# A gated recurrence inside a four-layer kernel: the PSUM tiles of its gates merged, three small jobs moved to other places and engines

## The chip, the cores and the metric

The kernel runs on one core of a Trainium2 chip. The metric is the device time of one execution in microseconds (us). A core has TensorE (PE, matrix products; PEld is its weight load), VectorE (DVE), ScalarE (ACT), GpSimd (POOL) and SyncE (SP, which issues transfers). Each engine takes its own instructions in the order in which the program gives them, and waits for other engines by semaphores.

## The reference

Four residual layers over an activation `x` of 16 x 256 x 512 (batch, time, features) with a mask `cond` of 16 x 512: `x` plus an attention (8 heads), plus a depthwise convolution of 16 taps whose taps are the mask's rows, plus a recurrence, plus an attention (16 heads). The change touches the recurrence, a GRU over 256 steps:

```
def cell(h, x):
    gi = x @ W_ih + b_ih
    gh = h @ W_hh + b_hh
    i_r, i_z, i_n = jnp.split(gi, 3, axis=-1)
    h_r, h_z, h_n = jnp.split(gh, 3, axis=-1)
    r = jax.nn.sigmoid(i_r + h_r)
    z = jax.nn.sigmoid(i_z + h_z)
    n = jnp.tanh(i_n + r * h_n)
    h_new = (1.0 - z) * n + z * h
    return (h_new, h_new)
```

A step needs the state of the step before, so the 256 steps run one after another. The state is 16 x 512 and W_hh is 512 x 1536, all in float32.

## The kernel before

The first attention runs up to about 480 us of the profile, the recurrence from there to about 1567 us, the second attention after it. Within the recurrence the order on every engine is that of the Python code (`manual_schedule`). The waits between engines are not in the code: the tile framework derives them from the tiles that each instruction reads and writes, and from their order.

**A step** (`step`, L1223). Features lie on partitions; `state_part` (L1209) multiplies the old state by one gate's share of W_hh. For each of four chunks `f` of 128 features, four products with 32 output partitions each (`j`) run side by side in the array. So one gate is 16 products, which the trace shows as 32 matmul instructions, and one step has three gates. Their sums go to three PSUM tiles `pr`, `pn`, `pz` of 128 x 128, of which there are two sets (`sets`, L1173): one set serves two steps, since the input's products for two steps are made at once. In program order a step is:

1. PE: r products into `pr`; ACT: sigmoid of `pr` (L1237); DVE: transposes the result (`rT`, L1238).
2. PE: n products into `pn`; DVE: transposes `pn` (`hT`, L1240), multiplies it with r (`rn`, L1241), adds the input's share (`pre`, L1242); ACT: tanh (L1244).
3. PE: z products into `pz`; DVE: transposes `pz` in two halves (`zT`, L1249); ACT: 1 - z in two halves (`omz`, L1251); DVE: `d`, `m`, and the new state into `hist` (L1252, L1254, L1255), in halves too, so that the next step's first products can begin with the first half.

**What the loop adds to a step** (L1291 to L1312), after it in program order:

- `input_part` (L1187): the products of the input with W_ih for the r and z gates of a later pair of steps, added into the other set: 16 products of 128 columns a step.
- After every second step, three ACT copies (L1299) put the biases into the set just used.
- `turned_part` (L1195): a sixteenth of the n gate's input products for the next 16 steps (a "part"), four products of 256 columns a step, into a PSUM tile `pt`. Two buffers of the pool `psw` are there for it; every fourth step ACT takes one to SBUF (L1207).
- `take` (L1179): in the last four steps of a part, one ACT copy each brings a later part's input into order (L1185, 64 copies in all).
- `add_part` (L1216): once a part is done, two DVE additions write its states plus its input into `xT` (L1221, 32 in all).
- `conv` (L555): two taps of the convolution layer a step on DVE (L558, 384 instructions in all), but in the step that holds the additions.
- After step 8, `projection` (L346) transposes the second attention's three weight matrices: 12 transpositions on PE (L343), each copied out of PSUM by ACT (L354), through the pool `psw`.

The lines outside of the recurrence that the prediction uses: L618 to L629 in the setup, where one PSUM tile `ps` ("places") is written by PE in columns 0 to 63 (L621), read there by DVE (L624), then written in columns 64 to 79 (L627); and L1520 with L1529 in the second attention, where PE writes two halves of one bank of the tile `SM` (through the helper at L1457) and ACT reads them half by half. `SM` is made as eight banks of 512 float32 columns.

Of the kernel before, what the change touches and what calls it, by code (L numbers as in the profile page):

```python
# [264 lines left out]
def tile_kernel(ctx: ExitStack, tc: tile.TileContext, x, cond, Wq0, Wo0, W_ih, W_hh, b_ih, b_hh,  # L265
# [35 lines left out]
    whh = cpool.tile([P, NT, 3 * T], F32, tag="whh", name="whh")  # L301


    gbias = cpool.tile([72, P], F32, tag="gbias", name="gbias")
    nbias = cpool.tile([P, NT], F32, tag="nbias", name="nbias")

    wih = cpool.tile([P, NT, 3 * T], F32, tag="wih", name="wih")
# [38 lines left out]
    def projection(psm, wnat, flat, padded, R, dk, name):  # L346

        if padded is not None:
            nc.vector.memset(padded, 0.0)
        for oc in range(KC):  # L350
            for kc in range(KC):
                ps = transposed(psm, wnat, oc, kc, f"{name}t{oc}{kc}")
                if flat is not None:
                    nc.scalar.copy(flat[:, kc, oc * P : (oc + 1) * P], ps[:, 0:P])  # L354
                if padded is not None:
                    nh = P // dk
                    dst = padded[:, kc, oc * nh * R : (oc + 1) * nh * R].rearrange("p (h r) -> p h r", r=R)
                    nc.vector.tensor_copy(dst[:, :, 0:dk], ps[:, 0:P].rearrange("p (h i) -> p h i", i=dk))
# [274 lines left out]
    bi = b_ih.rearrange("(g f j i) -> g j f i", g=3, f=NT, i=32)  # L633
    bh = b_hh.rearrange("(g f j i) -> g j f i", g=3, f=NT, i=32)
    for at_row, src, g in ((0, bi, GATE_R), (4, bh, GATE_R), (36, bh, GATE_N), (64, bi, GATE_Z), (68, bh, GATE_Z)):
        nc.sync.dma_start(out=gbias[at_row : at_row + 4].rearrange("r (f i) -> r f i", i=32), in_=src[g])
    nc.sync.dma_start(out=nbias, in_=b_ih[2 * T : 3 * T].rearrange("(f p) -> p f", p=P))

    together = nc.values_load(flag[0:1, 0:1], min_val=0, max_val=1)
# [514 lines left out]
    with ExitStack() as es:  # L1154
        gp = es.enter_context(tc.tile_pool(name="gru", bufs=2))
        gw = es.enter_context(tc.tile_pool(name="gruw", bufs=1))
        psg = es.enter_context(tc.tile_pool(name="psg", bufs=1, space=PSUM))
        psw = es.enter_context(tc.tile_pool(name="psw", bufs=2, space=PSUM))
        yw.append(gw.tile([P, NT, B, WIN], F32, tag="yw2", name="yw2"))


# [8 lines left out]

        sets = [[psg.tile([P, P], F32, tag=f"{n}{i}", name=f"p{n}{i}") for n in "rnz"] for i in range(2)]  # L1173
        bias = gw.tile([P, 3, P], F32, tag="bias", name="bias")

        def gates(w, f, j):
            return w[:, f].rearrange("p (g c j i) -> p g j c i", g=3, c=NT, i=32)[:, :, j]

        def take(p, f):  # L1179


            if f == 0:
                parts[p] = gp.tile([P, NT, PART, B], F32, tag="xw", name=f"xw_{p}", bufs=3)
            lo = p % 2 * PART
            nc.scalar.copy(parts[p][:, f], yw[p // 2 % 3][:, f, :, lo : lo + PART].rearrange("p b s -> p s b"))  # L1185

        def input_part(k, f, g):  # L1187

            xw, s0 = parts[2 * k // PART], 2 * k % PART
            x2 = xw[:, f, s0 : s0 + 2].rearrange("p s b -> p (s b)")  # L1190
            for j in range(4):
                nc.tensor.matmul(sets[k % 2][0 if g == GATE_R else 2][32 * j : 32 * j + 32].rearrange("p (f i) -> p f i", i=32),  # L1192
                                 lhsT=x2, rhs=gates(wih, f, j)[:, g], start=False, stop=False, skip_group_check=True)

        def turned_part(p, q):  # L1195

# [19 lines left out]
        def add_part(p, q):  # L1216
            dst = xT[:, :, :, p * PART + q : (p + 1) * PART : 2]
            at_col = B * ((q + 1) % 2)
            src = hist[p % 2][:, q::2, :, at_col : at_col + B].rearrange("p s f b -> p f b s")
            lo = p % 2 * PART  # L1220
            nc.vector.tensor_tensor(dst, yw[p // 2 % 3][:, :, :, lo + q : lo + PART : 2], src, ALU.add)  # L1221

        def step(t):  # L1223
            pr, pn, pz = sets[t // 2 % 2]
            before, slot = state(t - 1)
            after, _ = state(t)

            def mine(tl):
                return tl.rearrange("p (f r) -> p f r", r=2 * B)[:, :, B * (t % 2) : B * (t % 2) + B]

            def sbuf(name, shape):
                return gp.tile(shape, F32, tag=name, name=f"{name}_{t}")

            r, rT, hT, zT = (sbuf(n, [P, P]) for n in ("r", "rT", "hT", "zT"))
            rn, pre, nn, omz, d, m = (sbuf(n, [P, NT, B]) for n in ("rn", "pre", "nn", "omz", "d", "m"))
            state_part(slot, pr, GATE_R)
            nc.scalar.activation(r, pr, AF.Sigmoid)  # L1237
            nc.vector.transpose(rT, r)  # L1238
            state_part(slot, pn, GATE_N)
            nc.vector.transpose(hT, pn)  # L1240
            nc.vector.tensor_tensor(rn, mine(hT), mine(rT), ALU.mult)  # L1241
            nc.vector.tensor_tensor(pre, rn, turned[t // PART][:, :, t % PART], ALU.add)  # L1242
            state_part(slot, pz, GATE_Z)
            nc.scalar.activation(nn, pre, AF.Tanh)  # L1244


            halves = [slice(h * NT // 2, (h + 1) * NT // 2) for h in range(2)]
            for h in range(2):
                nc.vector.transpose(zT[:, h * P // 2 : (h + 1) * P // 2], pz[:, h * P // 2 : (h + 1) * P // 2])  # L1249
            for f in halves:  # L1250
                nc.scalar.activation(omz[:, f], mine(zT)[:, f], AF.Sigmoid, scale=-1.0)  # L1251
            nc.vector.tensor_tensor(d, nn, before, ALU.subtract)  # L1252
            for f in halves:
                nc.vector.tensor_tensor(m[:, f], d[:, f], omz[:, f], ALU.mult)  # L1254
                nc.vector.tensor_tensor(after[:, f], m[:, f], before[:, f], ALU.add)  # L1255
# [3 lines left out]

        taps = [(f, k, w * WIN) for w in range(EARLY // 2, D // WIN) for f in range(NT) for k in range(TAPS)]  # L1260
        parts, turned, added = {}, {}, 0

        n = TAPS - 1 + EARLY * PART
        room = yw[2].rearrange("p f b s -> p (f b s)")
# [2 lines left out]
        with tc.manual_schedule(engines=ENG):  # L1267

            nc.scalar.activation(gp.tile([P, NT], F32, tag="table", name="table", bufs=1), nbias, AF.Sigmoid)
            nc.gpsimd.tensor_copy(xs[:, :, TAPS - 1 :], xT[:, :, B - 1, 0 : EARLY * PART])  # L1270
            for w in range(1, EARLY):
                for _, _, f in early(B - 1, w, xs, products):
                    f()
            for t in hist:
                nc.gpsimd.memset(t, 0.0)
            nc.vector.tensor_copy(hist[1][:, PART - 1, :, 0:B], condT)
            for k in range(2):
                for ps, base in zip(sets[k], (0, 32, 64)):
                    nc.tensor.matmul(ps, lhsT=cst("gsel")[base : base + 8], rhs=gbias[base : base + 8], start=True, stop=True)
            for i, ps in enumerate(sets[0]):  # L1280
                nc.scalar.copy(bias[:, i], ps)
            for f in range(NT):
                take(0, f)
            xparts = [(f, g) for f in range(NT) for g in (GATE_R, GATE_Z)]
            for f, g in xparts:
                input_part(0, f, g)
            for q in range(PART):
                turned_part(0, q)
            for f in range(NT):
                take(1, f)  # L1290
            for t in range(D):  # L1291
                step(t)
                p, q = divmod(t, PART)
                if t + 2 < D:
                    for f, g in xparts[4 * (t % 2) : 4 * (t % 2) + 4]:
                        input_part(t // 2 + 1, f, g)
                    if t % 2:
                        for i, ps in enumerate(sets[t // 2 % 2]):
                            nc.scalar.copy(ps, bias[:, i])  # L1299
                if p + 1 < D // PART:  # L1300
                    turned_part(p + 1, q)
                if p + 2 < D // PART and q >= 12:
                    take(p + 2, q - 12)
                for _ in range(2):
                    if added // 2 < p:
                        add_part(*divmod(added, 2))
                        added += 1
                    elif taps:
                        conv(*taps.pop(0))
                if t == 8:  # L1310
                    for wnat, flat, name in zip(wnats, (wq3T, wk3T, wv3T), ("wq3", "wk3", "wv3")):
                        projection(psw, wnat, flat, None, R3, DK3, name)  # L1312
            for q in range(2):
                add_part(D // PART - 1, q)

# [429 lines left out]
```

## Time and profile before

| | us |
|---|---|
| median of three runs (lowest, highest) | 2416.81 (2415.17, 2427.05) |
| the profiled execution | 2425.97 |
| its span | 2424.2 |
| in it: from the first r sigmoid (L1237) to the last | 494.28 to 1563.81 |
| a step, r sigmoid to r sigmoid, median of 255 | 4.06 |
| the longest, step 8 to step 9 (the 12 transpositions) | 13.59 |
| busy time of PE, DVE, ACT, POOL between 494 and 1567 us | 1045.7, 870.7, 359.4, 0.0 |

In the profile's lines "engine line op out<-in shapes xcount" names a group of instructions; in the timeline the first two columns are the start and the length in us, and a bracket at the end tells how long the engine was idle before and which instruction ended the wait.

### The profile page before, as it was taken

How to read it: one execution, taken by the hardware profiler on the slowest of the kernel's cores; microseconds unless marked ns; L12 is line 12 of the kernel's file. 1: busy time of each engine (PE TensorE's matmuls, PEld its weight loads, DVE VectorE, ACT ScalarE, POOL GpSimd, SP SyncE). 2: the span in 40 equal slices, each digit the busy share in tenths (PEclk: the TensorE clock that was granted, in tenths of full speed). 3: DMA queues.
4: the chain of work that ended last, by engine and by line, in shares of the span. 5: the costliest groups of instructions: out<-in, count | busy, mean ns of one | idle time of the engine just before them, and what ended most of it. 6: DMA issues, size and time to landing. Idle time of an engine off the chain costs nothing.

```text
span 2424.2 us, 105987 instructions
## 1 busy us (share of the span) xinstructions
PE 2217.7 (91%) x47074; PEld 1451.9 (60%) x47074; DVE 1677.4 (69%) x4611; ACT 997.8 (41%) x2648; POOL 420.7 (17%) x428
## 2 busy tenths in 40 slices
PE   5999999499999999999999999749999999999994
PEld 3555554278988898888988888623333333333331
DVE  2378778768888888888888655626555666566661
ACT  3555554233333333333333333215545555455552
POOL 3244433300000000000000000140332224222213
PEclk8999999699999999999999999969999999999997
DMA  6223322400000000000000000010111111111101
GB/s 198 72 79 106 83 70 66 152 4 4 5 4 5 4 5 4 4 5 4 5 4 5 5 4 4 4 42 16 37 42 32 31 43 43 32 31 38 32 21 40
DMA packets 70172, 83.97 MB, mean 35 GB/s; under 512 B 28808, under 2 KB 48842, under 8 KB 69700
## 3 DMA queue, kind: packets, MB, share of 16 engines
q1 hardware_dynamic: 60484, 60.09, 8.6%
q0 software_dynamic: 9216, 16.96, 2.3%
q8 instruction: 373, 6.11, 1.1%
q14 instruction: 99, 0.81, 0.1%
HBM read 48.58 MB, written 35.98 MB: 35 GB/s over the span
## 4 chain that ended last, share of the span: by engine, by line
issue 46%; PE 45%; DMA 2%; DVE 2%; another core or an unknown queue 1%; POOL 1%; ACT 1%; SPq 1%; POOLq 0%; DVEq 0%; ACTq 0%
PE smC L1457 10%; PE smC L1584 8%; PE smA L830 6%; PE smC L1616 6%; PE smC L1641 5%; PE smA L984 3%; PE smA L1014 3%; PE smA L941 2%; PE smC L1507 1%; DVE nmC L1591 1%; PE smA L856 1%; DMA backA<-result,goto 1%; PE smA L883 1%; PE smA L917 1%
## 5 line engine op out<-in xcount | busy, mean ns | idle before, releaser
L1591 DVE TENSOR_REDUCE nmC<-smC 128x2 f32<-128x576 f32 x512 | 364.9, 752 | 243.4 <-PE smC L1584 193.4
L1627 ACT ACTIVATE wih<-smC 128x1024 f32<-128x1024 f32 x256 | 252.3, 1023 | 146.9 <-PE smC L1616 132.8
L1213 PE MATMUL pr<-whh,hist 128*32 128x128 f32 x8192 | 284.0, 275 | 11.9 <-DVE hist L1255 6.7
L1213 PE MATMUL pz<-whh,hist 128*32 128x128 f32 x8192 | 283.6, 273 | 2.3 <-issue 2.3
L1213 PE MATMUL pn<-whh,hist 128*32 128x128 f32 x8192 | 280.8, 273 | 0.0
L1213 PEld LDWEIGHTS pr<-whh,hist 128*32 128x32 f32 x8192 | 222.1, 110 | 97.0 <-DVE hist L1255 43.8
L558 DVE SCALAR_TENSOR_TENSOR yw<-xT,condT,yw 128x512 f32<-128x512 f32 x360 | 269.4, 748 | 6.8
L1213 PEld LDWEIGHTS pz<-whh,hist 128*32 128x32 f32 x8192 | 240.1, 110 | 4.2 <-issue 3.7
L1192 PE MATMUL pr<-wih,xw 128*32 128x128 f32 x4096 | 230.0, 274 | 11.1 <-issue 6.1
L1213 PEld LDWEIGHTS pn<-whh,hist 128*32 128x32 f32 x8192 | 239.2, 110 | 0.1
L1584 PE MATMUL smC<-kC,qC 32*128 32x288 f32 x2048 | 203.8, 460 | 31.2 <-ACT qC L1557 17.4
L1192 PE MATMUL pz<-wih,xw 128*32 128x128 f32 x4096 | 230.4, 274 | 2.0 <-issue 1.1
L1584 PEld LDWEIGHTS smC<-kC,qC 32*128 32x128 f32 x2048 | 86.1, 186 | 232.4 <-DVE nmC L1591 93.5
L1244 ACT ACTIVATE nn<-pre 128x64 f32<-128x64 f32 x256 | 65.7, 257 | 387.6 <-DVE pre L1242 387.6
L1237 ACT ACTIVATE r<-pr 128x128 f32<-128x128 f32 x256 | 71.1, 278 | 293.3 <-PE pr L1213 293.3
L1445 POOL MEMSET pbC<- 128x512 f32 x4 | 2.3, 616 | 1088.0 <-issue 1088.0
L1681 POOL TENSOR_TENSOR aC<-aC,pbC 128x512 f32<-128x512 f32 x64 | 81.6, 1282 | 591.0 <-DMA pbC<-sums 413.5
L1204 PE MATMUL pt<-xw,wih 128*32 128x256 f32 x2048 | 172.8, 382 | 0.1
L1616 PE MATMUL smC<-qC,kC 32*128 32x512 f32 x1024 | 162.9, 648 | 6.0 <-ACT e3C L1624 4.6
L1192 PEld LDWEIGHTS pr<-wih,xw 128*32 128x32 f32 x4096 | 146.9, 110 | 15.5 <-issue 14.8
L1192 PEld LDWEIGHTS pz<-wih,xw 128*32 128x32 f32 x4096 | 148.3, 110 | 6.1 <-issue 6.0
L313 POOL DMA_INDIRECT table<-xT,togo x128 | 128.3, 1002 | 89.6 <-ACT xT L860 59.9
(184 smaller groups left out, 3468.8 us busy)
## 6 DMA issues: line engine op xcount, KB each, us to landing
xA<-in_x_dram SPq DMA_DIRECT2D x16, 512.0 KB
pbC<-sums SPq DMA_DIRECT2D x256, 32.0 KB
out_dram<-oC SPq DMA_DIRECT2D x32, 256.0 KB
table<-zeros SPq DMA_DIRECT2D x16, 288.0 KB
pbA<-totals SPq DMA_DIRECT2D x120, 36.0 KB
xsA<-table SPq DMA_DIRECT2D x16, 256.0 KB
result<-ocA SPq DMA_DIRECT2D x16, 256.0 KB
xsC<-table SPq DMA_DIRECT2D x16, 256.0 KB
```

The source lines that it names most:

```text
L313: one = nc.gpsimd.indirect_dma_start(tables[b], bass.IndirectOffsetOnAxis(togo[:, f, b : b + 1], 0), xT[:, f, b], None, bounds_check=ROOM ...
L558: nc.vector.scalar_tensor_tensor(acc, xT[:, f, :, lo : lo + WIN], condT[:, f, k : k + 1], xT[:, f, :, t0 : t0 + WIN] if k == 0 else acc, A ...
L830: nc.tensor.matmul(to[r : min(n, r + R)], lhsT=left[:, r : min(n, r + R)], rhs=right, start=start, stop=stop, skip_group_check=True)
L1192: nc.tensor.matmul(sets[k % 2][0 if g == GATE_R else 2][32 * j : 32 * j + 32].rearrange("p (f i) -> p f i", i=32), lhsT=x2, rhs=gates(wih, ...
L1204: nc.tensor.matmul(ps[32 * j : 32 * j + 32], lhsT=wih[:, kc, 2 * T + fo * P + 32 * j : 2 * T + fo * P + 32 * j + 32], rhs=parts[p][:, kc]. ...
L1213: nc.tensor.matmul(ps[32 * j : 32 * j + 32].rearrange("p (f i) -> p f i", i=32), lhsT=slot[:, f], rhs=gates(whh, f, j)[:, g], start=False, ...
L1457: nc.tensor.matmul(to[R3 * j : R3 * j + R3], lhsT=left[:, R3 * j : R3 * j + R3], rhs=right, start=start, stop=stop)
L1584: nc.tensor.matmul(SM[:, st[j].i, 0:ROOM], lhsT=Q[qt.i][R * j : R * j + R, qc * P : (qc + 1) * P], rhs=K[kt.i][R * j : R * j + R, 0:ROOM], ...
L1591: nc.vector.tensor_reduce(NM[nm.i][:, qc, lo : lo + len(some)], SM[:, some[0] : some[-1] + 1, 0:ROOM], AX.X, ALU.max, negate=True)
L1616: nc.tensor.matmul(SM[:, st[j].i], lhsT=K[kt.i][r, kc * P : kc * P + P], rhs=Q[qt.i][r, :], start=True, stop=True)
L1627: nc.scalar.activation(E[e.i][:, lo : lo + len(some)], SM[:, some[0] : some[-1] + 1], AF.Exp)
L1641: nc.tensor.matmul(SM[R * j : R * j + R, acc.i], lhsT=V[v.i][:, c, 8 * (g // 2) + 2 * j + q], rhs=E[held[c].i][:, j], start=(c == 0), stop ...
```

## The change

- The three gates of a pair of steps share one PSUM tile of 128 x 512 (`set0`, `set1`); `bank(k, g)` gives a gate its 128 columns, in the order r, z, n. The order of the step's instructions stays.
- The r and z products of the input, side by side in that tile now, become one product of 256 columns.
- The biases come in by one matmul a set and one ACT copy of 384 columns after every second step.
- `take` goes to POOL from part 2 on, `add_part` goes to POOL for all parts.
- Two additions a part are no longer counted against the taps; taps are left out in two steps of each 32.
- The 12 weight transpositions come one to every second step from step 8 on, through a PSUM pool of their own (`pst`).

```diff
-    gbias = cpool.tile([72, P], F32, tag="gbias", name="gbias")
+    gbias = cpool.tile([72, 3 * P], F32, tag="gbias", name="gbias")
...
+        pst = es.enter_context(tc.tile_pool(name="pst", bufs=1, space=PSUM))
...
-        sets = [[psg.tile([P, P], F32, tag=f"{n}{i}", name=f"p{n}{i}") for n in "rnz"] for i in range(2)]
-        bias = gw.tile([P, 3, P], F32, tag="bias", name="bias")
+        sets = [psg.tile([P, T], F32, tag=f"set{i}", name=f"set{i}") for i in range(2)]
+        bias = gw.tile([P, 3 * P], F32, tag="bias", name="bias")
...
+        def bank(k, g):
+            return sets[k % 2][:, g * P : (g + 1) * P]
...
-            nc.scalar.copy(parts[p][:, f], yw[p // 2 % 3][:, f, :, lo : lo + PART].rearrange("p b s -> p s b"))
+            (nc.scalar.copy if p < 2 else nc.gpsimd.tensor_copy)(parts[p][:, f], yw[p // 2 % 3][:, f, :, lo : lo + PART].rearrange("p b s -> p s b"))
-        def input_part(k, f, g):
+        def input_part(k, f):
...
-                nc.tensor.matmul(sets[k % 2][0 if g == GATE_R else 2][32 * j : 32 * j + 32].rearrange("p (f i) -> p f i", i=32),
-                                 lhsT=x2, rhs=gates(wih, f, j)[:, g], start=False, stop=False, skip_group_check=True)
+                nc.tensor.matmul(sets[k % 2][32 * j : 32 * j + 32, 0 : 2 * P].rearrange("p (g f i) -> p g f i", g=2, i=32),
+                                 lhsT=x2, rhs=gates(wih, f, j)[:, 0:2], start=False, stop=False, skip_group_check=True)
...
-            nc.vector.tensor_tensor(dst, yw[p // 2 % 3][:, :, :, lo + q : lo + PART : 2], src, ALU.add)
+            nc.gpsimd.tensor_tensor(dst, yw[p // 2 % 3][:, :, :, lo + q : lo + PART : 2], src, ALU.add)
...
-            pr, pn, pz = sets[t // 2 % 2]
+            pr, pz, pn = (bank(t // 2, g) for g in (GATE_R, GATE_Z, GATE_N))
...
+        turns = [(wnat, flat, oc, kc, f"{name}t{oc}{kc}") for wnat, flat, name in zip(wnats, (wq3T, wk3T, wv3T), ("wq3", "wk3", "wv3"))
+                 for oc in range(KC) for kc in range(KC)]
...
             for k in range(2):
-                for ps, base in zip(sets[k], (0, 32, 64)):
-                    nc.tensor.matmul(ps, lhsT=cst("gsel")[base : base + 8], rhs=gbias[base : base + 8], start=True, stop=True)
-            for i, ps in enumerate(sets[0]):
-                nc.scalar.copy(bias[:, i], ps)
+                nc.tensor.matmul(sets[k][:, 0 : 3 * P], lhsT=cst("gsel")[0:72], rhs=gbias, start=True, stop=True)
+            nc.scalar.copy(bias, sets[0][:, 0 : 3 * P])
...
-                    for f, g in xparts[4 * (t % 2) : 4 * (t % 2) + 4]:
-                        input_part(t // 2 + 1, f, g)
+                    for f in range(2 * (t % 2), 2 * (t % 2) + 2):
+                        input_part(t // 2 + 1, f)
                     if t % 2:
-                        for i, ps in enumerate(sets[t // 2 % 2]):
-                            nc.scalar.copy(ps, bias[:, i])
+                        nc.scalar.copy(sets[t // 2 % 2][:, 0 : 3 * P], bias)
...
-                for _ in range(2):
-                    if added // 2 < p:
-                        add_part(*divmod(added, 2))
-                        added += 1
-                    elif taps:
+                while added // 2 < p:
+                    add_part(*divmod(added, 2))
+                    added += 1
+                for _ in range(2 if t % WIN > 1 or not t else 0):
+                    if taps:
                         conv(*taps.pop(0))
-                if t == 8:
-                    for wnat, flat, name in zip(wnats, (wq3T, wk3T, wv3T), ("wq3", "wk3", "wv3")):
-                        projection(psw, wnat, flat, None, R3, DK3, name)
+                if t >= 8 and t % 2 == 0 and turns:
+                    wnat, flat, oc, kc, name = turns.pop(0)
+                    nc.scalar.copy(flat[:, kc, oc * P : (oc + 1) * P], transposed(pst, wnat, oc, kc, name)[:, 0:P])
```

More of the change, by code (lines that the diff above doesn't have):

```diff
@@ L635, in tile_kernel @@
     for at_row, src, g in ((0, bi, GATE_R), (4, bh, GATE_R), (36, bh, GATE_N), (64, bi, GATE_Z), (68, bh, GATE_Z)):
-        nc.sync.dma_start(out=gbias[at_row : at_row + 4].rearrange("r (f i) -> r f i", i=32), in_=src[g])
+        nc.sync.dma_start(out=gbias[at_row : at_row + 4, g * P : (g + 1) * P].rearrange("r (f i) -> r f i", i=32), in_=src[g])
     nc.sync.dma_start(out=nbias, in_=b_ih[2 * T : 3 * T].rearrange("(f p) -> p f", p=P))
@@ L1277, in tile_kernel @@
             for k in range(2):
-                for ps, base in zip(sets[k], (0, 32, 64)):
-                    nc.tensor.matmul(ps, lhsT=cst("gsel")[base : base + 8], rhs=gbias[base : base + 8], start=True, stop=True)
-            for i, ps in enumerate(sets[0]):
-                nc.scalar.copy(bias[:, i], ps)
+                nc.tensor.matmul(sets[k][:, 0 : 3 * P], lhsT=cst("gsel")[0:72], rhs=gbias, start=True, stop=True)
+            nc.scalar.copy(bias, sets[0][:, 0 : 3 * P])
             for f in range(NT):
                 take(0, f)
-            xparts = [(f, g) for f in range(NT) for g in (GATE_R, GATE_Z)]
-            for f, g in xparts:
-                input_part(0, f, g)
+            for f in range(NT):
+                input_part(0, f)
             for q in range(PART):
```

## The prediction

> **What bounds the kernel now.** I first read the busy tenths over the whole span, to find which engine fills the recurrence:
>
> ```profile
> PE   5999999499999999999999999749999999999994
> ...
> PEclk8999999699999999999999999969999999999997
> ```
>
> PE is busy nine tenths and more in every slice from about 540 to 1500 us, at full clock. That says little of what ends a step, for PE also does the input's products in the time in which a step waits for its state. So I looked at the timeline of single steps, and chose one near the end of the recurrence (step 253), where the taps are used up and only the r and z input products are left beside the step:
>
> ```profile
> 1554.57 1.08 PE L1213 MATMUL pr<-whh,hist 128*32 128x128 f32 x32 [0.38 <-DVE m L1254]
> ...
> 1555.44 1.08 PE L1213 MATMUL pn<-whh,hist 128*32 128x128 f32 x32
> 1555.71 0.28 ACT L1237 ACTIVATE r<-pr 128x128 f32<-128x128 f32 x1 [1.67 <-PE pr L1213]
> ...
> 1556.31 1.08 PE L1213 MATMUL pz<-whh,hist 128*32 128x128 f32 x32
> 1556.58 0.32 DVE L1240 STREAM_TRANSPOSE hT<-pn 128x128 f32<-128x128 f32 x1 [0.25 <-PE pn L1213]
> ...
> 1557.45 0.38 DVE L1249 STREAM_TRANSPOSE zT<-pz 128x64 f32<-128x64 f32 x2
> 1557.51 0.26 ACT L1244 ACTIVATE nn<-pre 128x64 f32<-128x64 f32 x1 [1.53 <-DVE pre L1242]
> ...
> 1557.80 0.35 ACT L1251 ACTIVATE omz<-zT 128x32 f32<-128x32 f32 x2
> 1557.80 0.23 DVE L1252 TENSOR_TENSOR d<-nn,hist 128x64 f32<-128x64 f32 x1
> ...
> 1558.36 0.19 DVE L1255 TENSOR_TENSOR hist<-m,hist 128x32 f32<-128x32 f32 x1
> ...
> 1558.60 1.08 PE L1213 MATMUL pr<-whh,hist 128*32 128x128 f32 x32 [0.33 <-DVE hist L1255]
> ```
>
> What the reader is to see: n starts 0.87 after r (1555.44), z 0.87 after n (1556.31), and the next r 2.29 after z, when the first half of `hist` is there. The step is 0.87 + 0.87 + 2.29 = 4.03. The next step, without any input products, also takes 4.07 (pr at 1558.60 and at 1562.67), and the median of all 255 is 4.06. So **the recurrence is bound by the chain through the state**: three gates one behind the other on PE, then zT, omz, m and hist. The input products fill PE in the 2.29, and the taps fill DVE.
>
> The second thing to see is that r (1555.71 to 1555.99) and hT (1556.58 to 1556.90) read their PSUM tiles *while* PE already writes the next gate. After the change the next gate lies in the tile that is being read.
>
> **What the program does then.** The trace has this case in the setup. PE writes columns 0 to 63 of `places`, DVE reads them, PE writes columns 64 to 79:
>
> ```profile
> 14.74 0.22 DVE L624 TENSOR_TENSOR posT<-places,condT 128x64 f32<-128x64 f32 x1 [4.34 <-PE places L621]
> ...
> 15.02 0.39 PE L627 MATMUL places<-condT,C 128*128 128x16 f32 x1 [0.32 <-DVE posT L624]
> ```
>
> No column is shared and L627's inputs had been in use since 10.3 us, yet PE waited until the read was over (14.74 + 0.22) and began 0.06 later. The other way round, in the second attention:
>
> ```profile
> 1617.96 3.64 PE L1457 MATMUL smC<-wv3T,xkC 128*32 128x256 f32 x32
> ...
> 1621.71 0.65 ACT L1529 COPY whh<-smC 128x256 f32<-128x256 f32 x2 [7.42 <-PE smC L1457]
> ```
>
> The first half's products were done about halfway (its last matmul starts at 1619.26), but ACT read that half only after the second half's. So waits go by the whole bank, not by columns.
>
> **The change part by part.**
>
> *Three gates in one tile.* It adds two waits to each step, both on PE: n waits until r has been read, z until hT has been read. Behind each on PE's queue stand the rest of the step and the input products; PE takes them in order, so nothing fills the gap, and the chain above is what waits.
> - n: r starts 1.14 after pr's first matmul, takes 0.28, hand-over 0.05 to 0.06: 1.48 instead of 0.87, plus 0.61.
> - z: hT starts 1.14 after pn's first, takes 0.32, hand-over 0.06: 1.52 instead of 0.87, plus 0.65. Taps do not hold hT up: two take 1.53 and end about 1.7 after pr, while hT comes at 1.48 + 1.14 = 2.62.
>
> Together 1.26 a step; 256 x 1.26 = **322.6**. Bounds: hand-overs of 0.04 give 1.22 (312), a weight load of 0.03 to 0.05 behind each wait 1.35 (346). Something comes back behind z: rn, pre and tanh run earlier against zT, so tanh (1557.51 to 1557.77) no longer keeps ACT from omz; d still follows zT's second half. Between 0 and 0.1 a step; I take 0.04, **-10** (0 to -25).
>
> *Twelve transpositions.* Step 8 to 9 takes 13.59 against 4.05: the burst costs 9.5, because `pt` holds one of the two buffers and each transposition waits for the copy of the one before (0.69 apart). Spread out, each stands behind `turned_part` in the 2.29, of which z takes 0.87 and the input some 1.3; 0.1 to 0.3 stands out, twelve times: **-9.5 + 2.4**.
>
> *Additions to POOL.* Steps after a part's end are 0.33 longer, 16 times: **-5.3**. What comes for it: POOL's tensor_tensor of the same 512 elements takes 1.28 (L1681), but up to 1.9 if it suffers from the strides as DVE does (L1221 1.11 against 0.75 for a tap). It is off the chain, but DVE's two-input instructions can be held up: L1568, 0.29 as a rule, took 1.36 both times it began 0.11 to 0.13 after an L1681. With taps in the same step (some 6 parts) I put the delay at 1.1, in the other 10 at 0.3, the four `take` copies (0.4 each by L570) included: **+10** (0 to +40, were each of the 16 parts to lose two POOL instructions). After the last step POOL's queue has memsets and the sends of the second attention behind the additions: two of 1.28 instead of DVE's 2.0 for both, **+1** (0.5 to 3).
>
> *`take` and biases off ACT.* ACT is busy 359 of 1073 and not what ends a step; one copy for three and four copies a part fewer are worth nothing I can name.
>
> *One product for r and z.* It streams the same columns: 8 products of 256 for 16 of 128 in a step. A row for 256 columns exists, `pt`: groups of four start about 0.21 apart, as against 0.11 for 128. So nothing on PE's time, and it lies in the cover anyway. But PE gets 32 fewer instructions of 288 a step. Apart from burst and additions, 21 us are lost to steps in which PE stands with nothing awaited ("issue" in the waits, steps 7 to 15 of a part above all); with fewer instructions and 1.2 of standing time in each step I take **-12** (0 to -21).
>
> **Sum:** 322.6 - 10 - 9.5 + 2.4 - 5.3 + 10 + 1 - 12 = **+299** on the profiled execution's 2425.97. That one lies 9 above the median of the runs, which is what is predicted: 2416.8 + 299 = **2716**. A step should be near 5.27.
>
> *The clock.* It must hold at these pauses. In the burst it was halved from 533.6 to 540.4 us, though PE never paused over 0.36 there between matmuls. In steps without input products PE works 2.6 of 4.07 and the clock stayed at 1.00 (1558.6 to 1566.7); the new step has 3.9 of 5.27, more than that, so I leave it at 1.00.
> [...]
>
> **Rivals.**
> 1. *No wait: columns are kept apart when no matmul resets the bank.* For it: L627 starts a new sum (`start=True`), the step's products don't, and that might be what made PE wait there. Against: the reader at L1529 waited up to the very last matmul, which lies in other columns and resets nothing. Then only the small terms stay, the stalls at half: -9.5 + 2.4 - 5.3 - 10 + 5 + 1 = -16, **2400**, faster. It decides at a pn that starts before r ends. Chance 0.08, of it 0.03 within 0.5%.
> [...]
> 2. *One wait of the two costs nothing*, r's or hT's: 0.6 less a step, **2560**. Against: both stand on PE's queue between gates, and nothing else is between. 0.05.
> 3. *The clock falls:* the gates' 2.6 doubles, and the input products' 1.3 with it, which then outlasts the 2.29; some 9 a step, over **3600**. 0.03.
> 4. *The change doesn't do what it says* (additions or copies on POOL fall so far behind that steps wait for them): 4.2 to 6.4 of POOL work a part against 84; no room for it beyond the +40 above.
>
> **How the numbers follow.** Forecast 0.84. Its own bounds: low 312 - 25 - 9.5 + 1 - 5.3 - 21 + 0.5 = +253, 2670; high 346 - 9.5 + 4 - 5.3 + 40 + 3 = +378, 2795. Rivals 1 to 3 have 0.16 and stay outside; I widen the low end a little, to 2655. 0.5% is 12 us, about what a measurement of this kernel can tell from no change. Faster 0.05, same 0.03, slower 0.92.
>
> **What would show it.** In the profile after: PE idle before pn with ACT r as what ended it, and before pz with DVE hT, some 0.6 each, 256 times; a step near 5.27; no 13.6 step; PE's busy share down, and the clock at 1.00. Wrong would be a pn beginning before r's sigmoid is over (rival 1), POOL's additions over 2.5 long or DVE's small products near 1.3 in many steps (the lock mis-sized), or steps after a part's end over 7.

## The result, and the profile after

The changed kernel takes **2710.39 us** (median of four runs, 2695.31 to 2711.3) against 2418.09 for the kernel before beside it: ratio **1.119**, 95% interval 1.1138 to 1.1236, or 292 us more. The prediction was 2716.

In the two profiled executions the difference is 285.0 (2710.95 against 2425.97). Nearly all of it lies in the recurrence: from the first r sigmoid to the last it takes 1357.4 instead of 1069.5, +287.9. The part ahead of it is 1.4 shorter and the part behind it 1.6 shorter. The busy tenths of the changed kernel:

```profile
PE   6999995788888888888888888873899999999995
...
PEclk8999998899999999999999999997999999999997
```

PE's nines of the recurrence are eights now, and the recurrence fills 20.0 slices (of 67.7 us) instead of 17.6 (of 60.6). The granted clock is at half for 3.4 us in its first step (494.8 to 498.2 us; that step takes 1.6 longer than the median) and at 1.00 from there to its end. The timeline of one step of the changed kernel shows what PE no longer does (start, length; the bracket tells the idle time and what ended it):

```profile
900.36 1.08 PE L1217 MATMUL set<-whh,hist 128*32 128x128 f32 x32
...
901.51 0.28 ACT L1241 ACTIVATE r<-set 128x128 f32<-128x128 f32 x1 [0.46 <-PE set L1217]
...
901.84 1.08 PE L1217 MATMUL set<-whh,hist 128*32 128x128 f32 x32 [0.40 <-ACT r L1241]
...
902.99 0.32 DVE L1244 STREAM_TRANSPOSE hT<-set 128x128 f32<-128x128 f32 x1 [0.68 <-PE set L1217]
...
903.36 1.08 PE L1217 MATMUL set<-whh,hist 128*32 128x128 f32 x32 [0.44 <-DVE hT L1244]
...
904.51 0.38 DVE L1253 STREAM_TRANSPOSE zT<-set 128x64 f32<-128x64 f32 x2 [0.68 <-PE set L1217]
...
905.57 1.08 PE L1217 MATMUL set<-whh,hist 128*32 128x128 f32 x32
```

The n products (901.84) begin 0.05 after the r sigmoid's end, the z products (903.36) 0.05 after hT's. From r to n it is 1.48 (0.88 before), from n to z 1.52 (0.87 before), from z to the next r 2.23 (2.30 before): a step of 5.22 instead of 4.06. The view of PE's waits between 500 and 1840 us (total, times, longest) says that this happens in nearly every step (252 times in 1340 us, which hold some 256 steps):

```profile
PE set L1217 <- DVE hT L1244: 126.3, 252, 1.2
PE set L1217 <- ACT r L1241: 100.0, 252, 0.4
```

These totals are 0.50 and 0.40 for each wait. They fall short of the 0.65 and 0.60 in starts, since a matmul's modelled end lies behind the start of the next one as long as PE runs on (in the kernel before a gate's products show as 1.08, and the next gate's begin 0.88 after them).

The page's groups show two rows of the moved additions' cost (count, busy time, mean ns):

```profile
L558 DVE SCALAR_TENSOR_TENSOR yw<-xT,condT,yw 128x512 f32<-128x512 f32 x360 | 305.2, 848 | 6.8
...
L1225 POOL TENSOR_TENSOR xT<-yw,hist 128x512 f32<-128x512 f32 x32 | 70.3, 2197 | 1022.6 <-DVE hist L1259 1022.6
```

An addition takes 1.11 on DVE before. On POOL it takes 2.31 where DVE still has taps to do, and 1.86 in the last four parts, where none are left. A tap on DVE takes 0.85 on average instead of 0.75: those that start beside an addition (24, two in each of 12 parts) take up to 2.26.

To split the 255 steps, I call what a step takes over the median step its **excess**. Before it adds up to 33.2: 9.5 in the step with the 12 transpositions, 5.3 in the steps after those that hold additions, 17.1 in the odd steps of the second half of a part (PE "issue"; 1.3 of it belong to steps 7, 71, 135 and 199, in which PE waits for `hist`). After it is 25.3: 19.0 in the two steps around a part's end (POOL's additions), 4.1 in the 12 steps with a transposition, 1.6 in the first step (in part at half clock), and no "issue" in the odd steps of the second half.

### The profile page after: what moved, and what is told of

The parts are those of the page before. It is cut to its first block, busy times and chain, and to the rows that moved or that the text cites. A ratio compares the mean times of both kernels' runs of the same rounds, so it can differ in the third digit from the quotient of the medians.

```text
span 2709.2 us, 97565 instructions
## 1 busy us (share of the span) xinstructions
PE 2292.5 (85%) x42970; PEld 1312.2 (48%) x42970; DVE 1679.8 (62%) x4579; ACT 945.3 (35%) x2336; POOL 528.8 (20%) x516
## 4 chain that ended last, share of the span: by engine, by line
PE 79%; DVE 9%; ACT 4%; issue 3%; DMA 2%; another core or an unknown queue 1%; POOL 1%; SPq 1%; POOLq 0%; DVEq 0%; ACTq 0%
PE set L1217 28%; PE smC L1459 9%; PE smC L1586 7%; PE set L1196 7%; PE smC L1618 5%; PE smA L830 5%; PE smC L1643 4%; PE pt L1208 4%; DVE hT L1244 3%; PE smA L984 3%; DVE yw L558 3%; ACT r L1241 2%; PE smA L1014 2%; PE smA L941 2%
## 5 line engine op out<-in xcount | busy, mean ns | idle before, releaser
L1217 PE MATMUL set<-whh,hist 128*32 128x128 f32 x24576 | 830.9, 276 | 238.5 <-DVE hT L1244 128.1
L1217 PEld LDWEIGHTS set<-whh,hist 128*32 128x32 f32 x24576 | 624.6, 109 | 462.2 <-DVE hT L1244 196.8
L1196 PE MATMUL set<-wih,xw 128*32 128x256 f32 x4096 | 270.3, 382 | 18.5 <-DMA wv3nat<-in_L_cond_Wv_dram 18.5
L1253 DVE STREAM_TRANSPOSE zT<-set 128x64 f32<-128x64 f32 x512 | 97.3, 228 | 167.7 <-PE set L1217 167.6
L1683 POOL TENSOR_TENSOR aC<-aC,pbC 128x512 f32<-128x512 f32 x64 | 81.8, 1286 | 588.5 <-DMA pbC<-sums 365.3
L1244 DVE STREAM_TRANSPOSE hT<-set 128x128 f32<-128x128 f32 x256 | 79.9, 312 | 170.9 <-PE set L1217 170.9
L1196 PEld LDWEIGHTS set<-wih,xw 128*32 128x32 f32 x4096 | 128.6, 111 | 64.8 <-POOL hist L1281 19.6
L1255 ACT ACTIVATE omz<-zT 128x32 f32<-128x32 f32 x512 | 90.6, 224 | 166.1 <-DVE zT L1253 166.0
L1643 PE MATMUL smC<-wih,whh 128*32 128x512 f32 x1024 | 128.5, 617 | 8.8 <-DVE nmC L1593 5.8
L1242 DVE STREAM_TRANSPOSE rT<-r 128x128 f32<-128x128 f32 x256 | 78.3, 306 | 80.4 <-ACT r L1241 79.6
L948 DVE TENSOR_REDUCE whh<-smA 128x2 f32<-128x576 f32 x129 | 93.0, 748 | 49.8 <-PE smA L941 45.0
```

The costliest lines, as they stand in the source:

```text
L1196: nc.tensor.matmul(sets[k % 2][32 * j : 32 * j + 32, 0 : 2 * P].rearrange("p (g f i) -> p g f i", g=2, i=32), lhsT=x2, rhs=gates(wih, f, j ...
L1217: nc.tensor.matmul(ps[32 * j : 32 * j + 32].rearrange("p (f i) -> p f i", i=32), lhsT=slot[:, f], rhs=gates(whh, f, j)[:, g], start=False, ...
L1643: nc.tensor.matmul(SM[R * j : R * j + R, acc.i], lhsT=V[v.i][:, c, 8 * (g // 2) + 2 * j + q], rhs=E[held[c].i][:, j], start=(c == 0), stop ...
```

## Experiments

The runs fell on different chips. On two of them the kernel before takes 2333 and 2335, on the others 2417 to 2418; the difference lies ahead of the recurrence and behind it (last section). So each time is compared with the kernel before on its own chip, and the recurrence by its own length and step. Line numbers differ by a few from kernel to kernel.

**1. The merged tile alone.** The kernel before; only its three gates go into one tile, slices of which stand where the three tiles stood (and the biases are first put in by one matmul a set, ahead of the recurrence).

```diff
-        sets = [[psg.tile([P, P], F32, tag=f"{n}{i}", name=f"p{n}{i}") for n in "rnz"] for i in range(2)]
+        packs = [[psg.tile([P, 3 * P], F32, tag=f"rzn{i}", name=f"rzn{i}")] for i in range(2)]
+        sets = [[pk[0][:, 0 * P : 1 * P], pk[0][:, 2 * P : 3 * P], pk[0][:, 1 * P : 2 * P]] for pk in packs]
...
```

> [...] Theory (PE waits by the bank, twice a step, on the chain): pn 1.48 after pr, pz 1.52 after pn, pr 2.21 after pz as in the changed kernel, a step of 5.21; of the 34 us that steps lose to transpositions, additions and standing now only the transposition burst is left, so the recurrence takes 255 x 5.21 + 10 = 1340 instead of 1070, and the median is near 2418 + 270 = 2688. Rival (the loss comes from POOL's additions and copies, or from the 256-column products): a step of 4.06 and 2418.

Measured 2614.85 against 2332.92: ratio 1.120 (1.1184 to 1.1221), **+282**. Step 5.21, r to n 1.477, n to z 1.519. The merged tile by itself is as slow as the whole change. The excess is 13.4 (9.5 the transpositions): the additions, still on DVE, and PE's "issue" cost nothing in the long step.

**2. Each wait alone.** Two gates in a tile, the third in one of its own: r with n, then z with n (the edit from experiment 1 to the first of them; the other is made alike).

```diff
-        packs = [[psg.tile([P, 3 * P], F32, tag=f"rzn{i}", name=f"rzn{i}")] for i in range(2)]
+        packs = [[psg.tile([P, 2 * P], F32, tag=f"rn{i}", name=f"rn{i}"), psg.tile([P, 1 * P], F32, tag=f"z{i}", name=f"z{i}")] for i in range(2)]
...
```

> The kernel before with r and n in one tile and z in one of its own. Theory: the wait of n for r's sigmoid alone is there: pn 1.48 after pr instead of 0.87, pz 0.87 after pn as before, a step of 4.05 + 0.61 = 4.66; PE stands 0.6 a step, which takes up most of the 21 us of standing and the 5 us of the additions: 2418 + 156 - 25 = 2549. Rival (the two waits are not additive, one is hidden behind the other): either no change or all of the loss, 2418 or 2688.

> The kernel before with z and n in one tile and r in one of its own. Theory: the wait of z for hT alone is there: pz 1.52 after pn, pn 0.87 after pr; behind z some 0.08 comes back, because tanh is over before omz is due; a step of 4.05 + 0.57 = 4.62, and 2418 + 146 - 20 = 2544; steps with additions grow by 0.4, since hT now holds up PE and stands behind them on DVE. Rival as for the run with r and n: 2418 or 2688.

Timelines of PE in the kernel with r and n together, then in the one with z and n together:

```profile
900.78 1.08 PE L1214 MATMUL rn<-whh,hist 128*32 128x128 f32 x32
902.26 1.08 PE L1214 MATMUL rn<-whh,hist 128*32 128x128 f32 x32 [0.40 <-ACT r L1238]
903.16 1.06 PE L1214 MATMUL z<-whh,hist 128*32 128x128 f32 x32
```

```profile
903.86 1.08 PE L1214 MATMUL r<-whh,hist 128*32 128x128 f32 x32
904.73 1.08 PE L1214 MATMUL zn<-whh,hist 128*32 128x128 f32 x32
906.25 1.08 PE L1214 MATMUL zn<-whh,hist 128*32 128x128 f32 x32 [0.43 <-DVE hT L1241]
```

Only the gate that shares a tile with the one being read waits. r with n: 2453.39, ratio 1.051 (1.0492 to 1.0528), +120.5, step 4.59. z with n: 2471.88, ratio 1.059 (1.0572 to 1.0607), +139.0, step 4.69. Over the step of 4.06 that is 0.52 and 0.62, together 1.15, and both waits in one kernel (experiment 1) give 1.15. So the waits add up, and neither is free. Both sizes were missed by about a tenth: 131 was expected of r with n, and 126 of z with n. With r and n together, every step gives back 0.09 between z and the next r; with z and n together, only every second one does. Experiment 5 shows the source.

**3. The change without the shared n.** The changed kernel with n in a tile of its own; r and z go on sharing one, with their product of 256 columns.

```diff
-        sets = [psg.tile([P, T], F32, tag=f"set{i}", name=f"set{i}") for i in range(2)]
+        sets = [psg.tile([P, 2 * P], F32, tag=f"set{i}", name=f"set{i}") for i in range(2)]
+        sets_n = [psg.tile([P, P], F32, tag=f"n{i}", name=f"pn{i}") for i in range(2)]
...
-                        nc.scalar.copy(sets[t // 2 % 2][:, 0 : 3 * P], bias)
+                        nc.scalar.copy(sets[t // 2 % 2], bias[:, 0 : 2 * P])
+                        nc.scalar.copy(sets_n[t // 2 % 2], bias[:, 2 * P : 3 * P])
```

> The changed kernel with n in a tile of its own (r and z share one, with their common product; everything else as changed). Theory: z's only neighbour is r, whose read is over before z begins, so both waits are gone; a step is back at 4.06, PE's 256-column products cost nothing. What is left of the change: transpositions 0.35 in 12 steps, POOL's additions holding up the taps, 1 to 2 a part now that a step has less slack. 255 x 4.06 + 4 + 28 + 10 = 1077 instead of 1070, the median 2425, between 2405 and 2440. Rival (the 256-column product or POOL's work makes the loss): near 2700.

Measured 2339.43 against 2332.92: ratio 1.0026 (1.0017 to 1.0036), **+6.5** of the 292. Both waits are gone, since n lies between r and z: when z comes, r has long been read. The total was as expected, but made up otherwise: the step is 4.04 and the excess 37.6, which is what the two steps around a part's end have by themselves (the rest adds up to nothing). DVE and POOL in one of them:

```profile
999.61 0.74 DVE L558 SCALAR_TENSOR_TENSOR yw<-xT,condT 128x512 f32<-128x512 f32 x1
...
1000.38 2.24 DVE L558 SCALAR_TENSOR_TENSOR yw<-xT,condT,yw 128x512 f32<-128x512 f32 x1
1002.55 0.30 DVE L1243 STREAM_TRANSPOSE rT<-r 128x128 f32<-128x128 f32 x1
1002.78 0.27 DVE L1245 STREAM_TRANSPOSE hT<-pn 128x128 f32<-128x128 f32 x1
```

```profile
999.77 2.31 POOL L1226 TENSOR_TENSOR xT<-yw,hist 128x512 f32<-128x512 f32 x1 [3.02 <-DVE hist L1260]
```

POOL's addition ends at 1002.08. The tap that was started beside it ends 0.54 later, and takes 2.24 instead of 0.75; rT and hT stand behind it on DVE, and they are on the chain. The addition is held up too: it began 0.16 after the tap before (999.61) and takes 2.31. The same instruction of the changed kernel, its shortest, median and longest (ns), and one in a part without taps:

```profile
L1225 POOL TENSOR_TENSOR xT<-yw,hist x32: 1856/2307/2327, 573.1 to 1854.8; 128x512 f32<-128x512 f32 x32
```

```profile
1598.39 1.87 POOL L1225 TENSOR_TENSOR xT<-yw,hist 128x512 f32<-128x512 f32 x1 [8.34 <-DVE hist L1259]
```

So 0.45 of the 2.31 goes with the tap beside which it began. Which DVE instructions are held up, the changed kernel's trace shows. All 24 taps that begin beside an addition take 2.23 to 2.26 and end 0.54 to 0.55 after it; `pre`, in the 11 steps in which it begins beside one of POOL's input copies, takes 0.57 to 0.58 instead of 0.23 and ends 0.08 after the copy. Both read two inputs in SBUF. rT reads one: it begins beside an addition in 7 steps and beside a copy in 12, and takes 0.30 to 0.31 there, as in the others.

**4. The additions back on DVE.** First in the changed kernel (all gates in one tile), where an addition takes the place of a tap again; then in the kernel of experiment 3, one addition a step beside one tap, with the input copies back on ACT as well (the second edit shown is that kernel's).

```diff
-            nc.gpsimd.tensor_tensor(dst, yw[p // 2 % 3][:, :, :, lo + q : lo + PART : 2], src, ALU.add)
+            nc.vector.tensor_tensor(dst, yw[p // 2 % 3][:, :, :, lo + q : lo + PART : 2], src, ALU.add)
...
-                while added // 2 < p:
-                    add_part(*divmod(added, 2))
-                    added += 1
-                for _ in range(2 if t % WIN > 1 or not t else 0):
+                one = added // 2 < p
+                if one:
+                    add_part(*divmod(added, 2))
+                    added += 1
+                for _ in range(1 if one else 2):
```

> The changed kernel with the additions back on DVE and counted against the taps as before; the input copies stay on POOL. Theory (POOL's additions take 2.3 each and hold up the tap that DVE begins while one runs, and rT and hT stand behind the tap: 0.7 to 0.97 in two steps of each part that has taps): those 20 us go; two additions of 2.17 on DVE fit before hT, which comes 2.6 after pr now, so nothing comes in their place: 2710 - 20 = 2690. Rival (the long steps at a part's end come from the copies on POOL): no change, 2710.

> What the other runs point to: the changed kernel with n in a tile of its own, the additions back on DVE, one to a step beside one tap (instead of two in one step without taps), and the input copies back on ACT. It keeps the spread transpositions and the one product. Theory: steps at 4.06; the burst's 9.5 and the additions' 5.3 gone, 0.2 to 0.35 for each of 12 transpositions come for them, and half of the standing goes with PE's fewer instructions: 9.5 + 5.3 - 4 + 10 = 21 less, 2397 (2385 to 2410), faster than both. Rival (one addition and one tap do not fit before rT, or the transpositions cost what the burst did): 2410 to 2420, the same as before.

The first: 2613.37, ratio 1.120 (1.1181 to 1.1218), recurrence 1341.0. The changed kernel itself, run again with a profile on another chip:

> The changed kernel as it is, on the chip of the other runs. Theory: the recurrence keeps its 1357 us (step 5.22) and only the parts ahead of it and behind it are shorter there, by some 85 us in all, as in the other runs: near 2626, ratio 1.125; the additions on GpSimd then cost 1357 - 1341 = 16 us against the same kernel with the additions back on DVE (ratio 1.12 there). Rival: the recurrence is shorter there too (under 1345); then the additions cost nothing in the long step, and what looked like their price is the other chip.

It took 2712.04 against 2418.47 (1.1212, 1.1169 to 1.1256), not the 2626 that I had expected: that chip is one of the slower ones. Its recurrence was 1357.4 once more, so the additions on POOL cost 1357.4 - 1341.0 = **16** in the long step. The expected 20 did not go altogether, because the input copies are still on POOL: without additions ahead of them they now start beside taps, 21 of which take 1.01 to 1.18 instead of 0.75, and 3.2 of this kernel's excess of 9.1 lie in the steps with the first copies of a part (13, 29 and so on). The 19.0 of the two steps around a part's end less 3.2 is the 16.

The second: 2301.98, ratio 0.9865 (0.9849 to 0.9881), **-33**; its excess is -0.1. Against experiment 3 the moves back are worth 38 in the recurrence (1068.3 to 1030.3). That is the additions' doing: in experiment 3 no tap is longer beside a copy alone. It is more than twice as much as in the long step, where a part's two held-up steps have 0.69 and 0.97 of excess instead of 1.3 and 2.0. There hT comes 0.6 later after the step's start, and so much of a tap's delay would be hidden; that fits, but was not tested apart. Next to nothing is left of an addition's cost on DVE where it shares a step with one tap (0.14 in a step at most).

**5. The one product alone, and what shortens the step.** The kernel before with r and z in one tile, their input product in one, and nothing else.

```diff
-                nc.tensor.matmul(sets[k % 2][0 if g == GATE_R else 2][32 * j : 32 * j + 32].rearrange("p (f i) -> p f i", i=32),
-                                 lhsT=x2, rhs=gates(wih, f, j)[:, g], start=False, stop=False, skip_group_check=True)
+                nc.tensor.matmul(packs[k % 2][0][32 * j : 32 * j + 32].rearrange("p (g f i) -> p g f i", g=2, i=32),
+                                 lhsT=x2, rhs=gates(wih, f, j)[:, 0:2], start=False, stop=False, skip_group_check=True)
```

> The kernel before with r and z in one tile, n in its own, and one 256-column product for the input's r and z; nothing else. PE gets 256 instructions a step instead of 288. Theory (the 21 us of PE standing without a wait, in the later steps of a part, come from PE getting its instructions late): 10 to 20 us go, 2398 to 2408. Rival (they come from something else, such as a buffer or ACT's copies): 2418, and the steps 11, 13 and 15 of a part as long as before.

Measured 2304.94, ratio 0.988 (0.9864 to 0.9897), **-30**, more than expected. The excess of the odd steps went (17.1 to 3.4, of which 1.4 is again the wait for `hist` in four steps), but the median step also fell from 4.06 to 3.98, which I had not foreseen. What PE did behind `hist` shows it. First the weight loads of two successive steps of the kernel before, then the wait instructions of the same line (count; ns each; PEldq stands for the sequencer of PE's weight loads), before and in this kernel:

```profile
901.70 0.81 PEld L1213 LDWEIGHTS pr<-whh,hist 128*32 128x32 f32 x32 [0.38 <-DVE hist L1255]
...
905.74 0.36 PEld L1213 LDWEIGHTS pr<-whh,hist 128*32 128x32 f32 x13 [0.40 <-issue]
```

```profile
L1213 PEldq EVENT_SEMAPHORE  x128: 51/51/51, 490.1 to 1562.6; - x128
```

```profile
L1214 PEldq EVENT_SEMAPHORE  x1: 51/51/51, 455.0 to 455.0; - x1
```

In the records of the kernel before, no instruction that does work waits for more than one semaphore (8828 wait for one). In every second step of the kernel before, the r products have to wait for two engines: DVE (`hist`) and ACT (the sigmoid of the step before, which read `pr`). The second wait is an instruction of its own, and the products begin 0.146 after the half state's end instead of 0.055. Where r and z share a tile, z has waited for that sigmoid long before, and the second wait is gone. It is also gone with r and n together, but not with z and n together (x128 there): hence the 0.09 that experiment 2 gave back in one kernel and not in the other.

ACT has the same: in every odd step of the kernel before the tanh begins 0.06 later behind its input, and has an instruction ahead of it that only waits (127 of them). The tanh waits for DVE and, since its buffer is one of two that it wrote itself, for ACT. In this kernel there is none; the kernel of experiment 4 has them again. The difference between the two is the bias copies: three of 128 columns, or one of 256 and one of 128. So I gave the kernel of experiment 4 three:

```diff
-                        nc.scalar.copy(sets[t // 2 % 2], bias[:, 0 : 2 * P])
-                        nc.scalar.copy(sets_n[t // 2 % 2], bias[:, 2 * P : 3 * P])
+                        for g in (GATE_R, GATE_N, GATE_Z):
+                            nc.scalar.copy(bank(t // 2, g), bias[:, g * P : (g + 1) * P])
```

> This is the version with n in a tile of its own, the additions on DVE and the copies on ACT, with one edit: the biases go back into the banks by three copies of 128 columns instead of one of 256 and one of 128. Theory (a second wait): in every odd step of that version, and of the kernel before, the tanh stands behind a wait instruction of its own on ACT (its buffer, one of two, was last written by ACT itself), and starts 0.06 later after its input (1.80 against 1.74 after the r sigmoid); where three copies run, the last of them waits for ACT itself and the tanh of the next odd step needs no second wait. Expected: tanh 1.74 in even and odd steps, odd step 3.98 instead of 4.04, 128 x 0.06 = 8 us less than 2302: ratio 0.983. Rival: the 0.06 belongs to the bigger copy or to the even step's other work on ACT; then the odd steps stay at 4.04 or grow with the third copy, and the ratio is 0.9865 or above.

Measured 2376.23 against 2418.47: ratio **0.9823** (0.9793 to 0.9853). The tanh starts 1.74 after r in every step, and both odd and even steps take 3.98. Since this ran on another chip than experiment 4, I ran both beside each other:

> The version with n apart, additions on DVE, copies on ACT and two bias copies, beside the one with three bias copies, on one chip. Theory (a second wait ahead of the tanh in every odd step): odd step 4.04, even step 3.98, recurrence 1030; as before, some 33 us less than the kernel before. Rival: the difference between the two lay in the chips; then both take the same time here within 3 us.

> The same with three bias copies. Theory: odd and even step 3.98, recurrence 1022, 8 us less than the version with two copies on the same chip, some 41 us less than the kernel before. Rival: within 3 us of the version with two copies.

Two copies: 2392.26, ratio 0.9903 (0.987 to 0.9935), odd step 4.045, recurrence 1030.5. Three copies: 2382.76, ratio 0.9851 (0.9826 to 0.9875), odd step 3.986, recurrence 1022.8. That is 7.7 less in the recurrence (8 expected) and 9.5 less in the median, whose intervals overlap a little. The spans of the two profiled executions differ by 2.6 only (2388.8 and 2386.2): with three copies the part behind the recurrence took 867, as in its first profile, against 855 to 860 in the other kernels on such chips, at a granted clock of 0.97 to 0.98 in the second attention. Whether that is chance or follows from the denser recurrence stays open. ACT in two steps of the kernel with two copies, and of that with three:

```profile
903.77 0.26 ACT L1249 ACTIVATE nn<-pre 128x64 f32<-128x64 f32 x1 [1.53 <-DVE pre L1247]
...
907.75 0.26 ACT L1249 ACTIVATE nn<-pre 128x64 f32<-128x64 f32 x1 [1.47 <-DVE pre L1247]
```

```profile
901.25 0.26 ACT L1249 ACTIVATE nn<-pre 128x64 f32<-128x64 f32 x1 [1.47 <-DVE pre L1247]
...
905.24 0.26 ACT L1249 ACTIVATE nn<-pre 128x64 f32<-128x64 f32 x1 [1.47 <-DVE pre L1247]
```

With three, two copies write the same tile, so the third waits for ACT's own first one; from then on no wait for the older tanh is needed. That the waits are made up in this way is read from the order of the waits in the records; that the third copy takes the second wait off the tanh is shown. This kernel (n apart, one product for r and z, transpositions one to a step, additions on DVE, copies on ACT, three bias copies) beats both given ones: by 1.5 to 1.8% against the kernel before.

**6. The kernel before once more**, for a second profile of it.

> The kernel before as it is, on the chip of the other runs, for a profile of it there. Theory: recurrence 1069 us with a step of 4.06 as in the first profile, excess over the median step 33 us, and the 85 us of difference between the chips lie ahead of the recurrence and behind it: 2333 us. Rival: the recurrence differs there too, and then every comparison of recurrences between the chips moves by as much.

Measured 2413.38: it too ran on a slower chip, so the rival about the quicker chips stays untested by it (for the kernel of experiment 4, run on both, the recurrence is 1030.3 and 1030.5). Recurrence 1062.8 instead of 1069.5, at the same step of 4.06. The excess is 26.2 instead of 33.2, and most of the difference is that of the odd steps: 11.3 instead of 17.1. This "issue" loss varies from run to run, and the other terms hardly do (the transpositions 9.1 instead of 9.5).

Not tried: three gates in one tile without the waits. PE would write a tile that ACT and DVE read, with nothing to order them. So no run shows whether the chip would need the waits.

## Why the prediction was right, step by step

| Step of the sum | predicted | measured | by |
|---|---|---|---|
| n waits for r, z waits for hT, 256 times | +322.6 | +318.5 | 0.598 and 0.646 in the starts |
| comes back between z and the next r | -10 | -19.5 | 2.304 to 2.228 |
| burst of transpositions, then one to a step | -9.5 + 2.4 | -9.5 + 4.1 | excess |
| additions off DVE | -5.3 | -4.7 | excess |
| POOL holds DVE up | +10 | +19.0 | excess (16 by experiment 4, where the copies bring 3.2 back) |
| tail behind the last step | +1 | none seen | -1.6 for the whole part behind |
| PE's "issue" | -12 | -17.1 (-11.3 by the second profile), 1.3 of it no "issue" | excess |
| sum | +299 | +291 | +287.9 in the recurrence; the medians of the pieces don't add up exactly |

- **The main step was right** in mechanism and size: waits by the whole tile (each of these tiles has at most the 512 columns of a bank of `SM`, so tile and bank are not told apart here), one hand-over of 0.05 to 0.06 plus the reader's own time. Experiments 1 and 2 show it with nothing else changed, and experiment 3 takes it away again. Rival 1 (columns are kept apart) fell with it, rival 2 (one wait is free) with experiment 2, rival 3 (the clock) with the granted clock of 1.00 in all steps but the first, and rival 4 (POOL falls behind) with no step around a part's end over 6.3. The hand-over of 0.04 and the weight load of 0.03 to 0.05 in the bounds were my estimates, and no run shows them: in the changed kernel n begins 0.052 behind r's end and z 0.054 behind hT's, each with its first weight load within 0.002 of its first matmul.
- **"Something comes back behind z"** was right in sign, mis-sized, and its reason was mostly wrong. From zT to the half state's end it takes 1.03 with the gates apart and 1.01 with the early tanh of experiment 1: 0.02 of the 0.08. The rest is the second wait of the r products in every other step, worth about 0.09 there (experiment 5), and that of the tanh, which delays the next r by 0.08 where the tanh is late (from z to r 2.293 in the odd steps before, 2.212 in experiment 5's first kernel) and by 0.014 where it is early (2.228 in the odd steps of the changed kernel, 2.214 in the even ones). The "issue" in the bracket of `pr` was read without asking what it was.
- **"Additions to POOL"**: the term for DVE's hold-up was mis-sized by half. The 1.9 allowed for an addition is what it takes alone (1.86); beside taps it takes 2.31, since it is held up as well, which the prediction left out. A tap was held in two steps of each of 12 parts, not of six, mostly at 0.69 and 0.97 a step. The -5.3 that the move was to earn is real but owed to the longer step: in experiment 1 the additions, still on DVE, cost nothing either. So the move is a loss of 16 in the long step, and of 38 in the short one.
- **Transpositions**: the burst went as worked out, each single one stands out by 0.34 instead of 0.2.
- **"Issue"**: taken at -12, it went altogether. It goes with PE's instructions (experiment 5: the records show 240 a step, matmuls and weight loads, instead of 272; the prediction's 288 is a miscount, its 32 fewer is right) and also with idle time alone (experiment 1: all 272 still there). What PE stood for in these steps stays open.
- The errors of +9 on one side and of -9.5, -5 and -4 (the waits) on the other cancel in part. None is over 10 of 299, but that 2716 came within 6 of the median is partly luck.

## What to carry to other kernels

Put into one PSUM tile only what is written and read in separate phases: here r and z (never in use side by side) gain from sharing (a step of 3.98 instead of 4.06 in experiment 5's first kernel), and n between them pays for every neighbour with the reader's whole time, on the chain (0.52 and 0.62 a step). Before moving work to GpSimd, look at which DVE instructions with two SBUF inputs will run beside it and what is queued behind those: here a tap took 2.24 instead of 0.75, with rT and hT behind it. In a chain-bound loop count the waits of the instructions on the chain, too: a second wait is an instruction (0.09 on PE and 0.06 on ACT here), and may go if an earlier instruction on that engine has already waited for the same thing.

## What the runs showed of the hardware

- The same addition of 512 strided elements a partition takes 1.11 on DVE and 1.86 on POOL, and 2.31 on POOL when it begins beside a tap on DVE; POOL's contiguous multiplications of that size (L1683) take 1.28. The addition takes 1.68 times DVE's time on POOL without a tap beside it, and 2.07 times with one.
- A wait instruction ahead of a waiting one costs 0.09 on PE (51 ns in the records) and 0.06 on ACT (17 ns).
- The clock stayed at 1.00 with idle gaps of 0.40 and 0.44 in each step, but for 3.4 us at half in the first one.
- Chips differ outside of the recurrence: on the quicker ones the first r sigmoid comes at 458 to 461 and 807 to 811 follow the last, on the slower ones 485 to 499 and 855 to 867. In two stretches of 200 us of the second attention, from 200 us behind the last r sigmoid on, the granted clock was 1.00 with PE busy for 199 on a quicker chip (experiment 5's first kernel), and 0.97 to 0.98 with 190 to 192 on a slower one (the kernel before). In the recurrence it is 1.00 on both but for single drops of 3 to 10 us, and the kernel of experiment 4 takes 1030.3 there on a quicker chip and 1030.5 on a slower one.
